# Scores of two steps taken together, their maxima subtracted by four 32-row matmuls

## The chip, the core and the metric

The kernel runs on one core of a Trainium2 chip. The core has a matrix engine (TensorE, PE in the profile; PEld is its loading of stationary operands), a vector engine (DVE), a scalar engine (ACT), GpSimd (POOL) and SyncE (SP), which mostly issues transfers. Each has an instruction stream of its own, and they wait for each other through semaphores. Matmul results go to PSUM, which has eight banks per partition. The metric is the device time of one execution in microseconds (us).

## The reference

The program is a chain of four blocks, each added to its input after a layer norm: an attention, a mixture of experts, a second attention with a position bias, and a two-layer local-attention transformer. The change touches the first one only, here in short:

```python
x = L0_attn_x                                        # 2 x 1024 x 128, float32
n = layernorm(x)
Q = (n @ Wq.T).reshape(2, 1024, 8, 64)               # 8 heads of 64
K = (n @ Wk.T).reshape(2, 1024, 8, 64)
V = (n @ Wv.T).reshape(2, 1024, 8, 128)
attn = softmax(einsum('bnhr,bmhr->bhnm', Q, K))      # 1024 x 1024 per batch and head
x = x + layernorm(einsum('bhnm,bmhd->bnd', attn, V))
```

There is no scale and no mask in this attention. The softmax is taken as the exponential of the score less its row's maximum, divided by the sum of these exponentials.

## The kernel before

`phase1` computes this block. Operands are kept as a high and a low float16 part, so a product is three matmuls: high by high, high by low, low by high.

Heads are taken in pairs, since a head has 64 rows of contraction and two fit into the 128 partitions: `rows` (line 320) is rows 0 to 63 for head e=0 and 64 to 127 for e=1. There are two batches and four pairs per batch, which makes eight `pair`s; each has two halves of 512 queries, which makes 16 units `u`; each unit has eight steps, so there are 128 steps. The pieces of work are:

- `project` (line 293) makes Q or K of a pair: six matmuls of 512 columns into one PSUM tile `big`, an ACT pass for the high part and a DVE pass (line 272) for the low part, both reading that tile. `values_of` (line 306) makes V of a pair for 512 tokens: twelve matmuls of 256 columns into a `big` tile, then ACT (line 214) and DVE (line 215) in the same way.
- `maxima` (line 322) takes rough scores of 128 queries against 512 keys, for both heads, by one matmul per head (line 329) into a `big` tile, and DVE reduces it to negated row maxima (line 332). After the eighth, `negated` (line 336) combines the halves and writes them, divided by 64, to columns 0 and 64 of a mostly zero tile `mz`. `as_rows` (line 344) transposes `mz` by four matmuls with an identity and copies the result to `mrow`: head 0's negated maxima in row 0, head 1's in row 64, zeros elsewhere.
- `scores` (line 351) takes the scores of 128 keys (step j of the unit) against the 512 queries, for both heads: eight matmuls (line 360), in pairs of one per head. The last pair multiplies `ones` (64 everywhere) with `mrow` and so adds the negated maxima. ACT takes the exponential into `p` (line 364) and casts it to the high part in `hl` (line 366); POOL subtracts for the low part (line 367).
- `values` (line 370) multiplies the eight `hl` tiles of a unit with V for 128 queries of one head: 24 matmuls of 129 columns (lines 49 to 51) into the tile `pu`. `accumulate` (line 382) takes the reciprocal of the sums in column 128 (line 387) and adds the scaled result to `acc` (lines 390 and 392), both on DVE.

PSUM is divided so: three buffers of two banks for `big`, one bank for `pu`, one for `sm`. A buffer is taken again when its last reader is done. `p` has three buffers, `hl` eighteen.

The order is set by the loop at line 420. At step m it queues `scores` of m, then `maxima` so that they run 12 steps ahead, then `values` and `accumulate` of step m - 9, then at some m `as_rows` (m modulo 8 is 4), `project` (m modulo 16 is 1 or 3) and `values_of` (m modulo 16 is 13 or 15), and pieces of other work: the second batch's tokens, and from step 80 on the preparation of the second stage (`tick`). `queue` (line 144) makes everything that a call issues come, on each engine, after what the calls before it issued; within a call a scheduler sets the order. The nine steps after the 128th have only `values` and `accumulate`.

Of the kernel before, what the change touches and what calls it, by code (L numbers as in the profile page):

```python
# [10 lines left out]
F32 = mybir.dt.float32  # L11
F32R = mybir.dt.float32r
F16 = mybir.dt.float16
BF16 = mybir.dt.bfloat16
I32 = mybir.dt.int32
AF = mybir.ActivationFunctionType
ALU = mybir.AluOpType
# [12 lines left out]
class Core:  # L30
# [7 lines left out]
    def pool(self, name, bufs, side, **kw):  # L38
        return self.tc.tile_pool(name=name, bufs=bufs, side=side, reuse_waits="tile", **kw)
# [194 lines left out]
def phase1(k, X):  # L234
# [5 lines left out]
    nc, A = k.nc, k.A  # L240
    H, R = 8, 64
    QSCALE = 16.0
    MSCALE = 64.0
    with ExitStack() as es:
# [5 lines left out]
        pp = pool("p1p", 2)  # L250
# [4 lines left out]
        big = lambda: ps_big.tile([128, 2, 512], F32, name="big")  # L255
# [10 lines left out]
        mz = [wp.tile([128, 4, 128], F16, name=f"mz{i}") for i in range(2)]  # L266
        ones = wp.tile([128, 128], F16, name="ones")
# [6 lines left out]
        S = {}  # L274

        def tokens(b):
            xn = tp.tile([128, NT, D], F32, name="xn")
            xTh, xTl = x2.tile([128, N], F16, name="xTh"), x2.tile([128, N], F16, name="xTl")
            for c in range(2):
                src = X[:, NT * b + 4 * c : NT * b + 4 * c + 4, :]  # L280
                dst = [xn[:, 4 * c + t, :] for t in range(4)]
                if b:
                    yield from k.ln_steps(x2, dst, lambda t: src[:, t, :])
                    continue
                k.ln_to(x2, dst, lambda t: src[:, t, :], *k.ln_stats(x2, lambda t: src[:, t, :], 4, False))
                s = slice(512 * c, 512 * c + 512)
                hi, _ = k.split_r(xTh[:, s], xTl[:, s], k.transposed(ps_sm, xn, c))
                S["first"] = S.get("first", hi)
            for c in range(2 * b):
                yield from k.transposed_steps(ps_sm, xn, c, xTh, xTl)  # L290
            S["x", b] = xTh, xTl
# [28 lines left out]
        rows = (slice(0, 64), slice(64, 128))  # L320

        def maxima(n):

            u, i = n // 8, n % 8
            pair, t, c = u // 2, 4 * (u % 2) + i // 2, i % 2
            qh, kh = S["q", pair][0], S["k", pair][0]
            ps = big()
            for e, r in enumerate(rows):
                nc.tensor.matmul(ps[:, e, :], qh[r, 128 * t : 128 * t + 128], kh[r, 512 * c : 512 * c + 512], start=True, stop=True)  # L329
            if i == 0:  # L330
                S["n", u] = up.tile([128, 4, 2, 2], F32, name="nm")
            S["red"] = nc.vector.tensor_reduce(S["n", u][:, i // 2, c, :], ps, AX.X, ALU.max, negate=True)  # L332
            if i == 7:
                negated(u)

        def negated(u):

            nm = S.pop(("n", u))
            nb = up.tile([128, 4, 2], F32, name="nb")
            nc.vector.tensor_tensor(nb, nm[:, :, 0, :], nm[:, :, 1, :], ALU.min)  # L340
            nc.vector.tensor_scalar(mz[u % 2][:, :, 0:128:64], nb, 1.0 / MSCALE, None, ALU.mult)

        def as_rows(u):
            z = mz[u % 2]
# [5 lines left out]

        def scores(n):

            u, j = n // 8, n % 8
            pair, c = u // 2, u % 2
            (qh, ql), (kh, kl), m = S["q", pair], S["k", pair], S["m", u]
            ks, qs = slice(128 * j, 128 * j + 128), slice(512 * c, 512 * c + 512)
            st = big()
            for i, (l, r) in enumerate(((kh, qh), (kh, ql), (kl, qh), (ones, m))):
                for e, d in enumerate(rows):
                    nc.tensor.matmul(  # L360
                        st[:, e, :], l[d, :] if i == 3 else l[d, ks], r[d, :] if i == 3 else r[d, qs], start=i == 0, stop=i == 3
                    )
            p = pp.tile([128, 2, 512], F32, name="p", bufs=3)
            S["exp"] = nc.scalar.activation(p, st, AF.Exp, scale=QSCALE**-2)  # L364
            hl = pp.tile([128, 2, 2, 512], F16, name="hl", bufs=18)
            nc.scalar.copy(hl[:, 0], p)  # L366
            S["lo"] = nc.gpsimd.tensor_tensor(hl[:, 1], p, hl[:, 0], ALU.subtract)  # L367
            S["p", n] = hl

        def values(n):  # L370
            u, i = n // 8, n % 8
# [28 lines left out]
        steps = B * H // 2 * 16  # L400
# [19 lines left out]
        for m in range(steps + lag):  # L420
            if m == 0:
                while done < 8:
                    k.queue(maxima, done)
                    done += 1
                k.queue(as_rows, 0)
                k.behind(scaled, wvh, wvl, wv, VSCALE)
            if m < steps:
                k.queue(scores, m)
            if m == 12:
                k.side.append(tokens(1))  # L430
            while m == 49 and k.side:
                k.aside()
            if m == 101:
                projecting.close()
            while done < min(steps, m + 1 + ahead):
                k.queue(maxima, done)
                done += 1
            if 0 <= m - lag < steps:
                k.queue(values, m - lag)
                k.queue(accumulate, m - lag)  # L440
            if m % 8 == 4 and m + 4 < steps:
                k.queue(as_rows, m // 8 + 1)
            if m % 16 in (1, 3) and m // 16 + 1 < B * H // 2:
                k.queue(project, m // 16 + 1, m % 16 // 2)
            if m in (2, 4):
                k.queue(values_of, 0, m // 2 - 1)
            if m % 16 in (13, 15) and m // 16 + 1 < B * H // 2:
                k.queue(values_of, m // 16 + 1, m % 16 // 2 - 6)
            if k.side:
                k.aside()  # L450
            elif 80 <= m < 86 or m >= 101 and m % 2 == 0:
                k.queue(k.tick)
# [1041 lines left out]
def tile_kernel(ctx: ExitStack, tc: tile.TileContext, A, out, first=1, last=4):  # L1494
# [33 lines left out]
    k.exp_tables()  # L1528
    k.later = []
    gens = [f(k, X) for f in (phase1, phase2, phase3, phase4)[first - 1 : last]]  # L1530
    ready = [False] * len(gens)

# [145 lines left out]
```

## Time and profile before

| what | us |
|---|---|
| median of three runs (lowest, highest) | 1354.97 (1350.28, 1356.17) |
| the profiled execution | 1356.68 |
| its span, first to last instruction | 1354.9 |
| start to the first `values` | about 62 |
| first `values` to the end of the last | about 409 |
| the rest, stages two to four | about 884 |

| 62 to 471 us of the span | PE | PEld | DVE | ACT | POOL |
|---|---|---|---|---|---|
| busy us of 409 | 381.4 | 258.6 | 263.8 | 301.2 | 274.3 |

The mean granted TensorE clock was 0.98 of full speed in this stretch and 0.945 over the span. In the profile a line of the first kind names the source line, the engine, the operation, what it writes and reads by the program's names, shapes, and how often; then busy time, the mean duration in ns, and the engine's idle time just before with what ended it. A line in order of time has start and duration in us first. Matmuls overlap in the pipeline, so their starts, not their durations, tell how fast they follow each other. A form such as `64*128` after MATMUL gives the rows and columns of the array that the matmul uses.

### The profile page before, as it was taken

What the parts mean: (1) busy time and instruction counts of PE and PEld (TensorE: products, weight loads), DVE (VectorE), ACT (ScalarE), POOL (GpSimd) and SP (SyncE); (2) the same over time, 40 slices, a digit from 0 to 9 for tenths busy, and PEclk for the clock granted to TensorE, in tenths of its full rate; (3) what the DMA queues carried; (4) which work ended last, traced back from release to release, by engine and by line L of the source; (5) the groups of instructions that cost most, each with busy time, mean ns of one, the idle gap of its engine ahead of it and who ended that gap; (6) DMA issues with size and microseconds to landing.
All of it is one profiled execution on the core that took longest, in us unless ns stands there. A gap on an engine that the chain in (4) does not pass through costs nothing.

```text
span 1354.9 us, 28455 instructions
## 1 busy us (share of the span) xinstructions
PE 1162.4 (86%) x11558; PEld 716.5 (53%) x11558; DVE 982.3 (72%) x1970; ACT 958.2 (71%) x1481; POOL 842.6 (62%) x525
## 2 busy tenths in 40 slices
PE   4799999999897889887799998798668898998886
PEld 1366666666565646443355544343336565666564
DVE  6777666776674385989888789571578887888855
ACT  2777777787686364541898987789367788887755
POOL 1666667777665463733676768785577886666611
PEclk8899999999898999998999999898679899999999
DMA  2000000000000031300000013000157666555520
GB/s 77 1 2 2 2 2 1 2 17 18 1 1 2 18 131 32 112 13 4 3 5 3 5 38 73 1 21 1 24 94 163 122 119 106 103 99 100 106 59 16
DMA packets 123394, 57.59 MB, mean 43 GB/s; under 512 B 105568, under 2 KB 114800, under 8 KB 123264
## 3 DMA queue, kind: packets, MB, share of 16 engines
q1 hardware_dynamic: 121360, 54.50, 18.7%
q8 instruction: 90, 1.47, 0.4%
q10 hardware_dynamic: 1472, 1.09, 0.3%
q0 software_dynamic: 432, 0.20, 0.2%
q14 instruction: 40, 0.33, 0.1%
HBM read 21.69 MB, written 1.11 MB: 17 GB/s over the span
## 4 chain that ended last, share of the span: by engine, by line
PE 42%; DVE 29%; ACT 14%; issue 6%; POOL 4%; DMA 3%; SPq 0%; POOLq 0%; DVEq 0%; ACTq 0%
DVE mx L869 5%; PE big L360 5%; PE pu L49 4%; PE pu L51 3%; PE pu L50 3%; DVE nm L332 3%; PE pu L920 3%; ACT pt L898 2%; PE big L49 2%; PE big L51 2%; PE big L50 2%; PE bank L895 1%; PE bank L860 1%; PE big L656 1%; DVE ln_st L81 1%
## 5 line engine op out<-in xcount | busy, mean ns | idle before, releaser
L367 POOL TENSOR_TENSOR hl<-p,hl 128x1024 f16<-128x1024 f32 x128 | 274.0, 2143 | 142.8 <-ACT hl L366 116.2
L903 POOL TENSOR_TENSOR hl<-pt,hl 128x2048 f16<-128x2048 f32 (+1 forms) x48 | 164.4, 3432 | 78.1 <-ACT hl L902 68.4
L332 DVE TENSOR_REDUCE nm<-big 128x2 f32<-128x1024 f32 x128 | 155.2, 1220 | 32.3 <-PE big L329 31.6
L364 ACT ACTIVATE p<-big 128x1024 f32<-128x1024 f32 x128 | 130.9, 1023 | 52.4 <-PE big L360 51.6
L49 PEld LDWEIGHTS <-hl 128*128 128x128 f16 x1024 | 100.5, 98 | 75.7 <-DVE acc L392 43.6
L366 ACT CAST hl<-p 128x1024 f16<-128x1024 f32 x128 | 133.8, 1045 | 4.1
L869 DVE TENSOR_REDUCE mx<-bank 128x1 f16<-128x512 f32 (+3 forms) x157 | 102.1, 653 | 32.1 <-PE bank L860 16.4
L869 DVE TENSOR_REDUCE mx<-bankz 128x1 f16<-128x512 f32 (+3 forms) x147 | 96.6, 660 | 18.7 <-PE bankz L864 12.8
L898 ACT ACTIVATE pt<-bank 128x512 f32<-128x512 f32 (+1 forms) x172 | 97.0, 582 | 18.5 <-PE bank L897 11.1
L49 PE MATMUL pu<-V1h,hl 128*128 128x129 f16 x512 | 92.6, 224 | 12.4 <-DVE acc L392 11.7
L49 PE MATMUL pu<-V0h,hl 128*128 128x129 f16 x512 | 93.1, 224 | 10.8 <-DVE acc L392 9.5
L50 PEld LDWEIGHTS <-hl 128*128 128x128 f16 x1024 | 101.3, 99 | 0.0
L1221 POOL TENSOR_TENSOR rot<-rot,rn 128x512 f32<-128x512 f32 x64 | 66.3, 1056 | 55.8 <-DVE rn L1211 50.4
L51 PEld LDWEIGHTS <-hl 128*128 128x128 f16 x1024 | 100.5, 98 | 0.0
L1196 POOL TENSOR_TENSOR rot<-rot,t 128x512 f32<-128x512 f32 x64 | 84.1, 1326 | 20.2 <-DVE t L1190 20.1
L51 PE MATMUL pu<-V0h,hl 128*128 128x129 f16 x512 | 92.5, 223 | 0.0
L50 PE MATMUL pu<-V0l,hl 128*128 128x129 f16 x512 | 92.5, 222 | 0.0
L51 PE MATMUL pu<-V1h,hl 128*128 128x129 f16 x512 | 92.0, 222 | 0.0
L50 PE MATMUL pu<-V1l,hl 128*128 128x129 f16 x512 | 92.0, 221 | 0.0
L898 ACT ACTIVATE pt<-bankz 128x512 f32<-128x512 f32 (+1 forms) x132 | 76.8, 583 | 20.8 <-PE bankz L897 9.9
L88 POOL TENSOR_TENSOR ln_rstd<-ln_rs,nhalf 128x4 f32<-128x4 f32 (+2 forms) x29 | 32.8, 1135 | 81.4 <-DVE ln_rs L84 67.3
L895 PE MATMUL bank<-qst,kz 128*128 128x512 f16 (+3 forms) x218 | 68.1, 345 | 13.5 <-DVE mx L869 7.5
(412 smaller groups left out, 3730.9 us busy)
## 6 DMA issues: line engine op xcount, KB each, us to landing
sb<-sd SPq DMA_DIRECT2D x16, 512.0 KB, 4.4
Vs<-V SPq DMA_DIRECT2D x60, 130.0 KB, 2.4
work<-in_t_w SPq DMA_DIRECT2D x2, 512.0 KB, 3.5
out<-F SPq DMA_DIRECT2D x3, 256.0 KB, 2.3
X<-in_L_attn_x SPq DMA_DIRECT2D x2, 256.0 KB, 3.3
w<-in_t_wqk SPq DMA_DIRECT2D x1, 512.0 KB, 5.1
wv<-in_t_wv ACTq DMA_DIRECT2D x1, 512.0 KB
X<-in_L_attn_x ACTq DMA_DIRECT2D x1, 512.0 KB, 5.0
```

The source lines that it names most:

```text
L49: mm(out, lh, rh, start=start, stop=False, **kw)
L50: mm(out, lh, rl, start=False, stop=False, **kw)
L51: mm(out, ll, rh, start=False, stop=stop, **kw)
L332: S["red"] = nc.vector.tensor_reduce(S["n", u][:, i // 2, c, :], ps, AX.X, ALU.max, negate=True)
L364: S["exp"] = nc.scalar.activation(p, st, AF.Exp, scale=QSCALE**-2)
L366: nc.scalar.copy(hl[:, 0], p)
L367: S["lo"] = nc.gpsimd.tensor_tensor(hl[:, 1], p, hl[:, 0], ALU.subtract)
L869: S["max"] = nc.vector.tensor_reduce(out, ps[:, :, :n], AX.X, ALU.max, negate=True)
L895: nc.tensor.matmul(st[:, a, :w], kz[:, a0 + a, 128 * j : 128 * j + 128], q1[:, s : s + w], start=True, stop=not diag)
L898: S["exp"] = nc.scalar.activation(pt[:, a0 : a0 + m, :w], st[:, :, :w], AF.Exp)
L903: nc.gpsimd.tensor_tensor(hl[:, 1, :, :w], pt[:, :, :w], hl[:, 0, :, :w], ALU.subtract)
L1196: eng("ra" if j else "rb", i).tensor_tensor(rot[:, j], rot[:, j], t2[:, j], ALU.add)
```

## The change

`scores` is now called at even steps only and does the work of two. It takes two `big` tiles. First come the matmuls that put the negated maxima into them: for each head and each of the two steps one matmul of `ones` by `mrow` over 32 rows, rows 0 to 31 and 64 to 95 for the first step, 32 to 63 and 96 to 127 for the second, each group at its own row position of the array. Then come the six score matmuls of the first step, its exponential, cast and subtraction, and the same of the second step. For this `negated` writes each maximum twice, to columns 0, 32, 64 and 96 of `mz`, so that `mrow` has them in rows 0, 32, 64 and 96.

```diff
-            nc.vector.tensor_scalar(mz[u % 2][:, :, 0:128:64], nb, 1.0 / MSCALE, None, ALU.mult)
+            twice = mz[u % 2][:, :, 0:128:32].rearrange("p t (e i) -> p t e i", e=2)
+            nc.vector.tensor_scalar(twice, nb.unsqueeze(3).to_broadcast([128, 4, 2, 2]), 1.0 / MSCALE, None, ALU.mult)
...
-            ks, qs = slice(128 * j, 128 * j + 128), slice(512 * c, 512 * c + 512)
-            st = big()
-            for i, (l, r) in enumerate(((kh, qh), (kh, ql), (kl, qh), (ones, m))):
-                for e, d in enumerate(rows):
-                    nc.tensor.matmul(
-                        st[:, e, :], l[d, :] if i == 3 else l[d, ks], r[d, :] if i == 3 else r[d, qs], start=i == 0, stop=i == 3
-                    )
-            p = pp.tile([128, 2, 512], F32, name="p", bufs=3)
-            S["exp"] = nc.scalar.activation(p, st, AF.Exp, scale=QSCALE**-2)
-            hl = pp.tile([128, 2, 2, 512], F16, name="hl", bufs=18)
-            nc.scalar.copy(hl[:, 0], p)
-            S["lo"] = nc.gpsimd.tensor_tensor(hl[:, 1], p, hl[:, 0], ALU.subtract)
-            S["p", n] = hl
+            qs = slice(512 * c, 512 * c + 512)
+            st = [big() for _ in range(2)]
+            for e in range(2):
+                for i in range(2):
+                    d = slice(64 * e + 32 * i, 64 * e + 32 * i + 32)
+                    nc.tensor.matmul(st[i][:, e, :], ones[d, :], m[d, :], start=True, stop=False, tile_position=(d.start, 0))
+            for i in range(2):
+                ks = slice(128 * (j + i), 128 * (j + i) + 128)
+                for l, r in ((kh, qh), (kh, ql), (kl, qh)):
+                    for e, d in enumerate(rows):
+                        nc.tensor.matmul(st[i][:, e, :], l[d, ks], r[d, qs], start=False, stop=l is kl)
+                p = pp.tile([128, 2, 512], F32, name="p", bufs=3)
+                S["exp"] = nc.scalar.activation(p, st[i], AF.Exp, scale=QSCALE**-2)
+                hl = pp.tile([128, 2, 2, 512], F16, name="hl", bufs=18)
+                nc.scalar.copy(hl[:, 0], p)
+                S["lo"] = nc.gpsimd.tensor_tensor(hl[:, 1], p, hl[:, 0], ALU.subtract)
+                S["p", n + i] = hl
...
-            if m < steps:
+            if m < steps and m % 2 == 0:
                 k.queue(scores, m)
```

## The prediction

> **What bounds the kernel now.** I read the page first, then busy time by stretch, then the first stage in order of time, and the order in which the changed program's instructions stand. The page:
>
> ```profile
> span 1354.9 us, 28455 instructions
> ...
> PE 1162.4 (86%) x11558; PEld 716.5 (53%) x11558; DVE 982.3 (72%) x1970; ACT 958.2 (71%) x1481; POOL 842.6 (62%) x525
> ...
> L332 DVE TENSOR_REDUCE nm<-big 128x2 f32<-128x1024 f32 x128 | 155.2, 1220 | 32.3 <-PE big L329 31.6
> L364 ACT ACTIVATE p<-big 128x1024 f32<-128x1024 f32 x128 | 130.9, 1023 | 52.4 <-PE big L360 51.6
> L366 ACT CAST hl<-p 128x1024 f16<-128x1024 f32 x128 | 133.8, 1045 | 4.1
> ```
>
> The exponential (L364) waits for the scores matmuls and hardly anything waits for it. By stretches (columns: PE, PEld, DVE, ACT, POOL busy, granted clock, DMA share, GB/s) the middle of stage one is PE's, at the full clock:
>
> ```profile
> 240.00:320.00 80.00, 77.28 (x929) 50.55 (x928) 58.51 (x108) 64.96 (x72) 62.14 (x31) 1.00 0.05 15
> ```
>
> One step, in order of time (start, duration): end of one values block, scores, maxima, next values block.
>
> ```profile
> 305.20 0.22 PE L51 MATMUL pu<-V0h,hl 128*128 128x129 f16 x1
> 305.35 0.39 PE L360 MATMUL big<-qh,kh 64*128 64x512 f16 x2
> 305.58 0.38 PE L360 MATMUL big<-ql,kh 64*128 64x512 f16 x2
> 305.79 0.38 PE L360 MATMUL big<-qh,kl 64*128 64x512 f16 x2
> 306.01 0.38 PE L360 MATMUL big<-mrow,ones 64*128 64x512 f16 x2
> 306.23 0.38 PE L329 MATMUL big<-kh,qh 64*128 64x512 f16 x2
> 306.54 0.23 PE L49 MATMUL pu<-V0h,hl 128*128 128x129 f16 x1
> ```
>
> Starts tell the price, since durations overlap. Two 64-row matmuls share one slot of 0.217. A values block is 24 matmuls 0.0575 apart, 1.32 from first to last start. From 128 rows to 64, 0.15 pass where 0.0575 would do; back, 0.31 where 0.217 would do: each change of row tiling costs 0.093. The step is 1.32+0.15+0.66+0.22+0.31 = 2.66. Counted so from first to last values block, the stage is 377.0 of the measured 407.6; nearly all undisturbed steps fit within 0.02. The rest is waits, 18 of it in six steps where stage two's preparation sits in DVE's queue.
>
> What the step hides is seen where stage one ends and only values are left:
>
> ```profile
> 453.71 0.22 PE L51 MATMUL pu<-V1h,hl 128*128 128x129 f16 x1
> 453.97 0.17 DVE L387 RECIPROCAL ri<-pu 128x1 f32<-128x1 f32 x1 [5.09 <-PE pu L51]
> 454.18 0.35 DVE L392 SCALAR_TENSOR_TENSOR acc<-pu,ri,acc 128x128 f32<-128x128 f32 x1
> ...
> 454.58 0.23 PE L49 MATMUL pu<-V1h,hl 128*128 128x129 f16 x1 [0.65 <-DVE acc L392]
> ```
>
> `pu` has one buffer, so 0.87 lie between the last start of a values block and the next block's first. In the step above scores and maxima fill 1.34, more than 0.87.
>
> The release of a projection's PSUM buffer is the second thing hidden (here `values_of`; `project` releases by L272 at the same 3.84):
>
> ```profile
> 277.64 0.22 PE L51 MATMUL pu<-V0h,hl 128*128 128x129 f16 x1
> 277.69 0.27 PE L49 MATMUL big<-wvh,xTh 128*128 128x256 f16 x1
> ...
> 279.10 0.39 PE L360 MATMUL big<-qh,kh 64*128 64x512 f16 x2
> 279.20 1.01 ACT L214 CAST V1h<-big 128x1024 f16<-128x1024 f32 x1 [0.65 <-PE big L51]
> ...
> 280.25 1.23 DVE L215 TENSOR_TENSOR V1l<-big,V1h 128x1024 f16<-128x1024 f32 x1 [1.80 <-ACT V1h L214]
> ```
>
> It comes free at 281.48, 3.84 after the values block's last start; 3.90 with 0.06 to the waiting matmul.
>
> **The change part by part**, over the 59 two-step periods between the first and last values block.
>
> *The slot saved.* Two steps had two slots for `ones`·`mrow`; four 32-row matmuls side by side need one. But the scheduler has put all four next to each other in only 32 of the 59; in 27 the second step's two follow behind scores of the first. Saving 32×0.217 = 6.9. Bounds: 0 (four overlap no better than two) to 6.9; two 64-row matmuls do share a slot fully, so I take 6.9. PE's instruction count, and the six score matmuls per step, stay.
>
> *Row-tiling changes.* 32 rows are a third mode. A period with the four together gains one change (128-32-64-128), a split one three: 32+27×3 = 113; twelve fall away late, where a step has lost both scores and maxima. 101×0.093 = +9.4. No row of before shows 64 against 32; bounds 0 (+0) and 0.2 (+20), twice the row; I take the row of 64 against 128.
>
> The Trainium skill, "TensorEngine Tiling (Array Packing)", Key Properties, speaks against the change here: it says that changing the tiling mode, not just the tile, drains the array. The rows agree that a change costs, 0.093; the page prices nothing, so by its rule alone the sum would only gain a positive term of unknown size. "TensorE: Matmul & The Clock Gate", Part 3, gives 3.07 times for four row tiles instead of 4, by which (an estimate) the saving would be some 2 smaller. Neither figure is used below.
>
> *The accumulate wait.* Scores now stand before every second values block. In the other gap PE has only maxima, 0.15+0.31 = 0.46, and must wait till 0.87. By the new order: 37 gaps with maxima alone, 37×0.41 = 15.2; 12 with the four `as_rows` matmuls too (0.69 filled), 12×0.18 = 2.2; 3 with nothing, 3×0.81 = 2.4; the few others about 1.3. Together +21.1. DVE is no later than in the quoted row: the earlier reduction (1.22) ends under the values block, the next is queued behind the accumulate. Bounds: 0 and +21.1 (a wait can't be below the DVE chain).
>
> *The buffer wait.* `big` has three buffers. After a projection (14 `values_of`, 12 `project` in the counted part) the projection and both scores tiles now hold all three, so the following maxima waits for L215 or L272 on DVE. Before, a scores and a maxima tile had the other two. Scores begin 1.46 after the last values start; with two steps in one, maxima would come at 1.46+7×0.217+0.093 = 3.07 (5 cases) or, split, at about 3.47 (21 cases), and must wait to 3.90: 5×0.83+21×0.43 = +13.2. Where dearer tiling pushes scores later, this wait shrinks by as much. Bounds 0 and +19.6 (tiling at nothing). What it displaces: DVE's delay after projections and a maxima that waits for `kh` cost before 0.2 three times and 0.3 once in 16 steps; seven times 0.9 = -6.3, now under the later PE.
>
> *At nothing.* The wider `mz` write (8 to 16 elements, L341 takes 0.18, 16 times) lies on DVE behind a reduction. Exp and cast come in pairs, 4 x 1.03 in a 5.6 period: ACT has room; POOL needs 2×2.14 = 4.3. So the rings of `p` and `hl` wait for nothing new. What the second step's scores are moved past is one maxima and one values block on PE and, on ACT, the `mrow` cast, now 2.1 later; its reader comes four steps on, and its PSUM buffer is wanted only about when it ends. No DMA is moved. The nine steps before the first values block run at ACT's pace (2.07), 0±2. SP's order is unchanged. Some ten later instructions swap places with neighbours on ACT, DVE and POOL: 0±3.
>
> *Sum:* -6.9+9.4+21.1+13.2-6.3 = +30.5. All is on PE, whose last values block opens stage two (the chain runs `pu`, `acc`, then stage two's transfer), so the span takes it whole. The profiled execution took 1356.68 (span 1354.9, 1.8 around it): 1387.2. It stands 1.7 above the median shown, 1354.97, so 1385 beside that median.
>
> **Rivals.**
> - *Tiling dearer, or the four don't overlap* (then the change doesn't do what it says). No overlap: +6.9, 1392. At 0.2 a change +20.2 instead of +9.4, the buffer wait down by 7.2 (5×0.11+21×0.32): 1389. Both 1396. For it: 32-row mode is unseen. Against: 64 and 128 behave alike both ways.
> - *Cheaper.* Tiling at nothing alone: -9.4+6.4 = -3, 1382, as the buffer wait takes it back. Buffer wait hidden alone: 1372; both: 1362. For it: L215 follows an ACT cast that could run earlier if PE's projection does. Against: the 3.84 recurs after every projection.
> - *Not slower: DVE is never last.* Both waits that I add are for DVE's releases. If PE reached the second values block later than 0.87, and the maxima later than 3.90, both go: 30.5-34.3 = -3.8, 1351. It decides only where PE takes 0.41 more per period from elsewhere, or the reciprocal and accumulate land within 0.46. Against: eight gaps of 0.87 in a row after 453.
> - *The clock.* Between 900 and 1000 it was granted at 0.74 with PE busy 74.7; full, it would return up to 74.7×0.26 = 19: 1366. Nothing in the change touches that stretch.
>
> **How the numbers follow.** Forecast case 1385 (own range 1377 to 1393): 0.64. Dearer 0.14, cheaper 0.13, DVE never last 0.05, clock 0.04. Range 1367 to 1402: dearer's 1396 with the ±5 of swaps and start on top, and below the buffer wait gone with the same ±5; it drops the two last cases and the cheap end. About 0.5% (6.8) is what a measurement here tells from no change. DVE never last is split over same and faster; the cheap end adds to same: faster 0.03, same 0.06, slower 0.91.
>
> **What would show it.** Steps alternate: gaps from values to values of 0.87 with PE waiting for DVE `acc` some 60 times in stage one, against 8 now; maxima behind a projection waiting for the DVE halves of `V` and `q`/`k` about 26 times; where the four `ones` stand together, four starts at once, then 0.31 to the first scores. Stage one some 30 longer, the rest unmoved. Wrong if PE's idle time on `acc` stays near 21, if a 32-row change costs far from 0.093, or if later stages move by over 5.

## The result and the profile after

The changed kernel takes 1388.11 us (median of four executions, 1385.74 to 1391.24), the kernel before beside it 1354.72: 1.0253 times as long, 95% interval 1.0222 to 1.0285, slower. The forecast was 1385, in a range of 1367 to 1402. The profiled execution took 1387.85.

The page of the changed kernel, the rows that answer to those of before, and the first `values` matmul:

```profile
span 1386.1 us, 28456 instructions
...
PE 1180.1 (85%) x11558; PEld 722.1 (52%) x11558; DVE 1003.3 (72%) x1970; ACT 952.3 (69%) x1481; POOL 838.1 (60%) x525
...
L332 DVE TENSOR_REDUCE nm<-big 128x2 f32<-128x1024 f32 x128 | 154.7, 1218 | 39.7 <-PE big L329 39.4
L370 ACT ACTIVATE p<-big 128x1024 f32<-128x1024 f32 x128 | 130.5, 1020 | 65.2 <-PE big L368 62.8
...
L49 PE MATMUL pu<-V1h,hl 128*128 128x129 f16 x512 | 92.6, 224 | 23.5 <-DVE acc L398 22.8
```

The counts are the same to one instruction: no matmul was saved, only placed side by side. L49 now sits idle for the accumulate. The same stretch that was shown of before, then the whole stage, and who PE waits for in it:

```profile
240.00:320.00 80.00, 74.64 (x851) 47.76 (x849) 58.80 (x101) 56.72 (x64) 52.44 (x27) 1.00 0.03 8
```

```profile
62.00:503.00 441.00, 391.54 (x4573) 259.24 (x4570) 285.04 (x510) 297.58 (x326) 270.57 (x135) 0.98 0.01 4
```

```profile
PE pu L49 <- DVE acc L398: 37.4, 58, 8.0
PE big L329 <- DVE V1l L215: 2.4, 6, 0.6
```

and the first of these of before:

```profile
PE pu L49 <- DVE acc L392: 21.2, 16, 5.2
```

(The columns are us in total, times, the longest.) In 80 us PE starts 851 matmuls instead of 929, at the full clock still. The wait for `acc` came 58 times instead of 16. The list has 21 waits of the maxima for the low halves of V, q and k; that of before has none. (In these totals, busy time runs to the modelled end of a matmul and covers part of a wait; I therefore measure waits by starts.)

The measure used from here on is the **gap**: from the last start of one values block to the first start of the next. There are 127, numbered by the block that they follow; even numbers lie behind a block of an odd head (e=1), before one of an even head, and hold what the odd step queues. Sums over gaps, in us, with `project` and `values_of` gaps apart, and those with n mod 16 = 3, in which DVE has `negated`; gaps 95 and later, where stage two's preparation runs beside, are a column of their own:

| | behind an odd head (47) | behind a projection (24) | n mod 16 = 3 (6) | other (17) | gaps 95 to 127 | stage |
|---|---|---|---|---|---|---|
| before | 75.3 | 65.7 | 8.5 | 22.7 | 64.4 | 408.9 |
| changed | 41.4 | 101.1 | 17.1 | 38.6 | 70.5 | 441.3 |

The stage is 32.3 longer. The first values block starts 1.7 later, and what follows the stage takes 880.8 instead of 883.6, so the span grows by 31.2. Over all profiled executions of this study that last part, whose code is the same in all kernels, took between 874 and 888; a single span is therefore read stage by stage, and times are compared by medians.

A two-step period with the four `ones` together, in order of time:

```profile
278.07 0.22 PE L51 MATMUL pu<-V1h,hl 128*128 128x129 f16 x1
278.22 0.39 PE L363 MATMUL big<-mrow,ones 32*128 32x512 f16 x4
278.55 0.39 PE L368 MATMUL big<-qh,kh 64*128 64x512 f16 x2
278.77 0.38 PE L368 MATMUL big<-ql,kh 64*128 64x512 f16 x2
278.99 0.38 PE L368 MATMUL big<-qh,kl 64*128 64x512 f16 x2
279.20 0.38 PE L368 MATMUL big<-qh,kh 64*128 64x512 f16 x2
279.42 0.38 PE L368 MATMUL big<-ql,kh 64*128 64x512 f16 x2
279.64 0.38 PE L368 MATMUL big<-qh,kl 64*128 64x512 f16 x2
279.89 0.39 PE L329 MATMUL big<-kh,qh 64*128 64x512 f16 x2
280.36 0.23 PE L49 MATMUL pu<-V1h,hl 128*128 128x129 f16 x1
```

Four matmuls start as one and hold one slot; from them to the first scores 0.33 pass where a slot is 0.217. The gap shown lasts 2.29, since its accumulate ended late on DVE; undisturbed, such a gap is 2.10, and 2.52 where the scheduler split the four. The gap just before it, behind an odd head:

```profile
275.88 0.22 PE L51 MATMUL pu<-V1h,hl 128*128 128x129 f16 x1
...
276.03 2.13 POOL L373 TENSOR_TENSOR hl<-p,hl 128x1024 f16<-128x1024 f32 x1 [2.58 <-ACT hl L372]
276.04 0.39 PE L329 MATMUL big<-kh,qh 64*128 64x512 f16 x2
276.14 0.17 DVE L393 RECIPROCAL ri<-pu 128x1 f32<-128x1 f32 x1 [0.26 <-PE pu L51]
276.35 0.35 DVE L398 SCALAR_TENSOR_TENSOR acc<-pu,ri,acc 128x128 f32<-128x128 f32 x1
...
276.75 0.23 PE L49 MATMUL pu<-V1h,hl 128*128 128x129 f16 x1 [0.33 <-DVE acc L398]
```

That is 0.87, with one maxima in it and PE waiting for DVE; 50 of the 59 odd-head gaps of the two-step periods are exactly so. And behind a projection:

```profile
295.86 0.22 PE L51 MATMUL pu<-V0h,hl 128*128 128x129 f16 x1
295.92 0.27 PE L49 MATMUL big<-wvh,xTh 128*128 128x256 f16 x1
...
297.43 1.01 ACT L214 CAST V1h<-big 128x1024 f16<-128x1024 f32 x1 [1.18 <-PE big L51]
...
298.48 1.23 DVE L215 TENSOR_TENSOR V1l<-big,V1h 128x1024 f16<-128x1024 f32 x1 [1.80 <-ACT V1h L214]
...
299.16 0.59 PE L368 MATMUL big<-qh,kl 64*128 64x512 f16 x2
...
299.76 0.39 PE L329 MATMUL big<-kh,qh 64*128 64x512 f16 x2
...
300.08 0.23 PE L49 MATMUL pu<-V0h,hl 128*128 128x129 f16 x1
```

The last row of scores starts at 299.16 (its second matmul at 299.37); the maxima come at 299.76, 0.05 after L215 is done with the projection's buffer (298.48+1.23) and 3.90 after the values block. With 0.32 to the next block the gap is 4.21 or 4.22, the same in every one of the 24 gaps of the table, whether the four `ones` are together or split. That is how a wait for a fixed event looks.

### The profile page after: what moved, and what is told of

Read it like the earlier page. It is cut to its first block, busy times and chain, and to the rows that moved or that the text cites. A ratio compares the mean times of both kernels' runs of the same rounds, so it can differ in the third digit from the quotient of the medians.

```text
span 1386.1 us, 28456 instructions
## 1 busy us (share of the span) xinstructions
PE 1180.1 (85%) x11558; PEld 722.1 (52%) x11558; DVE 1003.3 (72%) x1970; ACT 952.3 (69%) x1481; POOL 838.1 (60%) x525
## 4 chain that ended last, share of the span: by engine, by line
PE 44%; DVE 29%; ACT 14%; issue 6%; POOL 4%; DMA 2%; SPq 0%; POOLq 0%; DVEq 0%; ACTq 0%
PE pu L49 5%; DVE mx L875 5%; PE pu L51 4%; PE pu L50 4%; PE big L368 3%; PE pu L926 3%; ACT pt L904 2%; PE big L49 2%; DVE nm L332 2%; DVE acc L398 2%; PE big L51 2%; PE big L50 2%; PE big L662 2%; PE bank L866 1%; PE bank L901 1%
## 5 line engine op out<-in xcount | busy, mean ns | idle before, releaser
L373 POOL TENSOR_TENSOR hl<-p,hl 128x1024 f16<-128x1024 f32 x128 | 270.8, 2137 | 173.3 <-ACT hl L372 148.3
L332 DVE TENSOR_REDUCE nm<-big 128x2 f32<-128x1024 f32 x128 | 154.7, 1218 | 39.7 <-PE big L329 39.4
L370 ACT ACTIVATE p<-big 128x1024 f32<-128x1024 f32 x128 | 130.5, 1020 | 65.2 <-PE big L368 62.8
L49 PEld LDWEIGHTS <-hl 128*128 128x128 f16 x1024 | 100.7, 98 | 70.5 <-DVE acc L398 52.1
L49 PE MATMUL pu<-V1h,hl 128*128 128x129 f16 x512 | 92.6, 224 | 23.5 <-DVE acc L398 22.8
L49 PE MATMUL pu<-V0h,hl 128*128 128x129 f16 x512 | 93.5, 225 | 16.4 <-DVE acc L398 14.6
L1227 POOL TENSOR_TENSOR rot<-rot,rn 128x512 f32<-128x512 f32 x64 | 66.3, 1056 | 57.8 <-DVE rn L1217 50.2
L908 ACT CAST hl<-pt 128x2048 f16<-128x2048 f32 (+1 forms) x48 | 77.6, 1616 | 1.6 <-PE pu L926 0.2
```

What stands on the lines that cost most here:

```text
L49: mm(out, lh, rh, start=start, stop=False, **kw)
L370: S["exp"] = nc.scalar.activation(p, st[i], AF.Exp, scale=QSCALE**-2)
L908: nc.scalar.copy(hl[:, 0, :, :w], pt[:, :, :w])
```

## The experiments

The theory is that of the prediction: two waits, for the accumulate and for a projection's buffer, cost the time; the 32-row tiles themselves are nearly neutral. The rivals are that the tiles cost it, or that pairs of steps do through their bursts on ACT, POOL and DVE. Stage sums of all runs, in the columns from above:

| run | odd head | projection | mod 3 | other | 95 on | stage | ratio to before (95%) |
|---|---|---|---|---|---|---|---|
| e1_after_noacc | 28.1 | 102.6 | 19.3 | 39.4 | 64.4 | 427.6 | 1.0126 (1.0102 to 1.0149) |
| e2_before_noacc | 69.4 | 65.9 | 8.5 | 22.7 | 54.8 | 391.9 | 0.9915 (0.9893 to 0.9937) |
| e3_before_32 | 74.6 | 67.2 | 9.1 | 24.5 | 63.2 | 410.8 | 0.9998 (0.9980 to 1.0016) |
| e4_after_64 | 41.6 | 101.1 | 15.8 | 37.6 | 70.5 | 440.2 | 1.0248 (1.0221 to 1.0276) |
| e5_after_lo | 42.2 | 90.6 | 17.1 | 38.4 | 69.3 | 430.3 | 1.0177 (1.0156 to 1.0198) |
| e6_after_best | 47.1 | 77.5 | 19.4 | 34.3 | 83.3 | 434.3 | 1.0272 (1.0250 to 1.0293) |
| e7_after_apart | 57.1 | 101.1 | 11.2 | 24.8 | 63.3 | 429.9 | 1.0179 (1.0159 to 1.0198) |
| e8_after_apart2 | 63.5 | 66.3 | 11.2 | 25.1 | 68.9 | 408.0 | 0.9979 (0.9967 to 0.9991) |
| e9_best_cut | 51.6 | 75.9 | 17.4 | 33.0 | 63.0 | 412.8 | 1.0042 (1.0026 to 1.0057) |
| e10_after_cut | 65.2 | 66.4 | 9.1 | 24.8 | 63.5 | 401.3 | 0.9973 (0.9960 to 0.9986) |

### The accumulate, taken away in both kernels

```diff
-            ri = up.tile([128, 1], F32, name="ri")
-            nc.vector.reciprocal(ri, po[:, D : D + 1])
...
+            if e == 0:
+                ri = up.tile([128, 1], F32, name="ri")
+                nc.vector.reciprocal(ri, po[:, D : D + 1])
...
```

The reciprocal and the accumulate of odd heads are left out, in the changed kernel (first text) and in the kernel before (second).

> The changed kernel without the accumulation of the odd heads: the reciprocal and the scaled add of every first values block of a period are left out, so that the second block's matmuls no longer wait for DVE. The odd heads are missing from the sum, so the output is not the reference's. Theory (the wait for the one pu buffer, 0.87 from values to values, is the largest term): stage one 25 shorter than in the changed kernel, about 1363, and the gaps with maxima alone fall from 0.87 to 0.46. Rival (the loss is in the 32-row tiling and the buffers): within 4 of 1388, since neither is touched.

> The kernel before with the same accumulations of the odd heads left out (output not the reference's). Theory: only the last eight values blocks, which stand without cover, gain, four of their gaps by 0.65, and some 3 from DVE's delays: 1349 to 1353. Rival (DVE's load as a whole sets the stage, so less DVE work is worth as much here as in the changed kernel): about 1330.

Measured: 1369.62 against 1350.69 for the kernel before, and 1340.93. The plain odd-head gaps of the changed kernel fell from 0.87 to 0.47 or 0.48, as expected, and the gaps behind projections stayed at 4.21. But the time fell by less than foreseen: the odd-head gaps of the whole stage gave back 23.0 (13.3 up to gap 94, 9.7 after it), the others took 8.1 again, the values blocks 1.2, and the stage won 13.7. The kernel before won more than foreseen, 17.0 in its stage, nearly all in delays behind DVE: 1.51 became 1.34 in odd-head gaps next to projections, and gaps 95 to 127 lost 9.6. So this edit takes DVE work away beside the wait, which both kernels profit from, and the difference of the two times doesn't isolate the wait. The gaps show that the wait is there; its price needs another edit (e7).

### The tiles alone

```diff
+            for e in range(2):
+                d = slice(64 * e, 64 * e + 32)
+                nc.tensor.matmul(st[:, e, :], ones[d, :], m[d, :], start=True, stop=False, tile_position=(d.start, 0))
-            for i, (l, r) in enumerate(((kh, qh), (kh, ql), (kl, qh), (ones, m))):
+            for l, r in ((kh, qh), (kh, ql), (kl, qh)):
```

One step at a time as before, `ones` first and as two 32-row matmuls (above). And the reverse, pairs of steps as in the changed kernel with `ones` as 64-row pairs (below).

```diff
-                    d = slice(64 * e + 32 * i, 64 * e + 32 * i + 32)
-                    nc.tensor.matmul(st[i][:, e, :], ones[d, :], m[d, :], start=True, stop=False, tile_position=(d.start, 0))
...
             for i in range(2):
+                for e, d in enumerate(rows):
+                    nc.tensor.matmul(st[i][:, e, :], ones[d, :], m[d, :], start=True, stop=False)
```

> The kernel before with its two ones-by-mrow matmuls taken over 32 rows at row positions 0 and 64, and put first; one step at a time as before. It adds one change of row tiling per step, 128 in all, and saves nothing. Theory (a change to or from 32 rows costs what 64 against 128 costs, 0.093 to 0.10): 128x0.098 = 12.6 longer, 1367. Rival cheaper (free): 1355. Rival dearer (0.2): 1380.

> The changed kernel with its four ones-by-mrow matmuls as two pairs of 64 rows, as before the change, and mz with two columns; two steps are still taken together. It loses the saved slot (33x0.217 = 7) and gains back about 120 tiling changes (12), while the maxima after projections wait about 7 longer for their buffer: within 3 of the changed kernel's 1388, 1389 by the sum. Rival (32-row tiles cause the loss): 1355 to 1362.

Measured: 1350.33 against 1350.69, no change, and 1385.55, as slow as the changed kernel. In the first, an undisturbed gap went from 1.34 to 1.44: the change from 32 to 64 rows costs 0.10, as estimated. But 128 such steps would make 12.8, and the stage grew by 1.9: gaps with a wait for DVE in them absorbed it (1.51 to 1.44) or lost the wait (gap 109, 3.82 to 1.22). My theory had the mechanism and missed that cover. In the second, the plain gaps that hold the scores are 2.20, those behind an odd head 0.87 and the ones behind projections 4.21 as ever. The four-tile form is worth nothing here either way; taking two steps together costs the time. The rival of the tiles falls.

### The projection's buffer

```diff
-            scaled(hi, lo, flat(ps), QSCALE / VSCALE)
+            nc.scalar.activation(hi, flat(ps), AF.Copy, scale=QSCALE / VSCALE)
+            nc.vector.tensor_tensor(lo, hi, hi, ALU.subtract)
```

The same is done in `values_of`.

> The changed kernel, with one thing left out: the low half of the projections and of the values is written as zero (high half minus itself), so the second reader of a projection's buffer, on VectorE, is gone and the buffer comes free when ScalarE has read it. The instructions on TensorE stand in the same order. Theory (the maxima after 25 projections and value projections wait for VectorE to finish with the buffer): the gap from the values block before a projection to the next one, 4.21 us in 25 places in the changed kernel, falls to what TensorE needs there by the order of its instructions, about 3.4 where the four `ones` matmuls lie together and 3.8 where they are split, a sum of 11 to 13; the time falls from 1388 to 1375-1379, 1.015-1.018 of the kernel before. Rival (the gap is TensorE's own, or set by ScalarE's read): the gaps stay within 0.1 of 4.21 and the time within 3 of 1388. The 0.87 of the odd heads stays in both.

Measured: 1376.74, a ratio of 1.0177, as expected. The 24 gaps behind projections went from 4.21 or 4.22 to between 3.40 and 4.04, and their sum fell by 10.5; those behind an odd head did not gain (42.2 against 41.4), so it is not DVE's lighter load as such. The one shown above became:

```profile
288.07 0.22 PE L51 MATMUL pu<-V0h,hl 128*128 128x129 f16 x1
...
290.68 0.70 DVE L320 TENSOR_TENSOR V1l<-V1h 128x1024 f16<-128x1024 f16 x1 [1.80 <-ACT V1h L319]
...
291.37 0.59 PE L370 MATMUL big<-qh,kl 64*128 64x512 f16 x2
...
291.58 0.59 PE L331 MATMUL big<-kh,qh 64*128 64x512 f16 x2
...
292.10 0.23 PE L49 MATMUL pu<-V0h,hl 128*128 128x129 f16 x1
```

The row of the maxima (L331 here) follows the last row of scores by a slot, 0.21, instead of 0.60. The gap is 4.03 and not the expected 3.8, all of it PE's own: in this split order two slots hold one matmul each. The buffer wait is shown, and its price: 1388.11 less 1376.74 are 11 (10 by the ratios) of the 33, against 13.2 in the sum.

### Both waits covered by order alone

First, both maxima of a pair in the odd step, and the quads (the four `ones` matmuls of two steps) kept in line, with nothing between them:

```diff
-                k.queue(scores, m)
+                k.queue(lambda m: k.in_line(scores, m, line="scores"), m)
...
-            while done < min(steps, m + 1 + ahead):
+            while (m % 2 or m == 0) and done < min(steps, m + 1 + ahead):
```

> The changed kernel with two changes of order: the maxima of both steps are put into the odd step, behind the values of the even head, and the eight matmuls of a pair of `ones` are kept in one line, so that all 64 quads lie side by side. Everything is computed. Theory (the loss is two waits, for the accumulate of the even head with only one maxima in between, and for the buffer of a projection with the maxima right behind it): with two maxima in the gap before the odd head TensorE needs 0.68 of the 0.87 there, 0.19 is left 51 times over (10 in sum against 27 in the changed kernel); the buffer wait goes, since the maxima come one values block later; all 64 pairs save a slot of 0.217, or 14 in sum. By the same tally as in the prediction the stage is 2.5 longer than in the kernel before, 34 shorter than in the changed kernel: 1350-1358, 0.998-1.004 of the kernel before. Rival (taking two steps together costs through something else: the bursts on ScalarE, POOL and VectorE): 1370 or more.

(What this text and the next call the gap before the odd head, and the even head's accumulate, is the gap behind the odd head, and its accumulate.)

Measured: 1389.24, as slow as the changed kernel. The theory missed this outright. Block by block, though, it holds for most of the stage: up to block 90 the run is 5.7 later than before, where the changed kernel is 24.6 later (both from the first values block). It loses in two other places. The first block starts 6.8 later (what delays it stays open), and gaps from 95 on sum to 83.3 instead of 64.4. The largest, gap 109, 8.54 against 3.82 before:

```profile
444.04 0.22 PE L51 MATMUL pu<-V0h,hl 128*128 128x129 f16 x1
...
446.75 0.95 POOL L549 MEMSET work<- 128x1024 f32 x1 [1.33 <-DVE rank L547]
...
447.68 4.20 POOL L373 TENSOR_TENSOR hl<-p,hl 128x1024 f16<-128x1024 f32 x2
447.74 4.19 DVE L551 TENSOR_SCALAR work<-rank 128x64 f32<-128x64 f32 x2 [1.05 <-POOL work L549]
...
451.85 0.21 DVE L552 TENSOR_TENSOR work<-sc,work 128x64 f32<-128x64 f32 x1
451.99 0.15 DVE L393 RECIPROCAL ri<-pu 128x1 f32<-128x1 f32 x1
452.18 0.35 DVE L398 SCALAR_TENSOR_TENSOR acc<-pu,ri,acc 128x128 f32<-128x128 f32 x1
...
452.58 0.29 PE L49 MATMUL pu<-V0h,hl 128*128 128x129 f16 x1 [6.59 <-DVE acc L398]
```

Two operations of stage two on DVE, of 64 columns each, take 4.19 together; they start as POOL begins two subtractions back to back and end as these end. The accumulate is queued behind them, and PE behind the accumulate. This is a third cost, not among my steps.

Second, the quads stay, but the second step's scores go back to the odd step (`scored` holds the six score matmuls, exponential, cast and subtraction of one step):

```diff
             if m < steps and m % 2 == 0:
-                k.queue(scores, m)
+                k.queue(lambda m: k.in_line(scores, m, line="scores"), m)
+            if m < steps:
+                k.queue(scored, m)
```

and, in a further run, the maxima of the even steps behind a projection are put off:

```diff
-            while done < min(steps, m + 1 + ahead):
+            while (m == 0 or m % 16 not in (0, 2, 4, 14)) and done < min(steps, m + 1 + ahead):
```

> The four `ones` matmuls of two steps are taken together as in the changed kernel, kept in one line, but the scores of the second step, its exponentials and splits go back to the odd step; the second tile waits in its buffer with the maxima in it. Everything is computed. Theory: six matmuls of scores are again in the gap before the odd head, so the accumulate wait is gone (0.87 becomes about 1.12, TensorE's own work); a slot of 0.217 less in 64 places and a change to 32 rows of 0.10 more in 64 make 7 less than the kernel before; but the maxima now follow even closer behind a projection (one step's scores instead of two), so the buffer wait of 3.90 binds in 26 places for 38 in sum: 31 longer than the kernel before, 1378-1388, 1.017-1.026 of it. Rival (no buffer wait, or the maxima slip behind the wait): 1340-1350, 0.993-1.000.

> As the run with the second step's scores put back in the odd step, and in the even steps that follow a projection or a value projection the maxima are put off to the odd step. Everything is computed. Theory: neither the accumulate wait nor the buffer wait is left; a slot of 0.217 less in 64 pairs and a change to 32 rows of 0.10 more, 7 less than the kernel before: 1341-1347, 0.990-0.997 of it, the fastest of all runs that compute everything. Rival (the slot saved is covered by waits on VectorE, as the price of 32-row tiles was when it was paid alone): 1348-1356. Rival (holding the second tile's buffer over a values block costs a new wait on ScalarE): 1360 or more.

Measured: 1377.12 and 1350.45. They are the cleanest test, since everything is computed and only order moves. In the first, undisturbed gaps behind an odd head are 1.12 and the others 1.45: the accumulate wait is gone, and the stage is 11.4 shorter than the changed kernel's, while the gaps behind projections stand at 4.21 unmoved. The time is a shade below the expected 1378; the stage's +21 against the 31 of the tally is again the cover of waits for DVE: beyond the undisturbed length of each gap, the first 94 gaps hold 12.5 in before and about 4 here. In the second, these gaps fall to 2.54, but for most of those with n mod 16 = 11, which are 3.5 since `nb` is held under POOL there; the stage loses another 21.9, and it is 0.9 shorter than before. The time is above the expected 1341 to 1347 and where the first rival put it. Until block 80 it is 7.7 ahead, of which slots and changes make 4.7 (40×0.117); the rest is that PE waits less for DVE than in before. Then it loses 7 in gaps 83 to 109, the two largest of them (83, 3.54 against 1.37, and 109, 6.67 against 3.82) to DVE operations held under POOL like those above.

### Single steps where stage two runs beside

```diff
+    CUT = 88
...
-            if m < steps and m % 2 == 0:
+            if m < CUT and m % 2 == 0:
```

From step 88 on each step opens its own tile with two 32-row matmuls, and the maxima go back to every step. This is put on the run with both maxima in the odd step, and on the fastest one.

> The run with both maxima in the odd step and all quads in line, up to step 88; from there on one step at a time as in the kernel before (its `ones` as two 32-row matmuls in front, which cost nothing when they were paid alone). Everything is computed. Theory (two steps at a time cost what the tally says while TensorE sets the pace, and lose their time where the next stage's small VectorE operations run beside, each held as long as POOL's two subtractions that now come back to back): the first 80 values blocks stay at 4 to 5 more than in the kernel before, the last 48 lose nothing more instead of 21, the start keeps its 7: 1360-1368, 1.006-1.012 of the kernel before. Rival (the last blocks are late whatever form the scores have there): within 5 of the 1389 of the run without the cut.

> The fastest form so far (quads of `ones` in line, the second step's scores in the odd step, the maxima put off behind projections), up to step 88; from there on one step at a time as in the kernel before. Everything is computed. Theory: the 7.7 that the first 80 values blocks won stay, and the 7 that the last 40 blocks lost in two waits for VectorE behind POOL (6.67 and 4.05 us) are not lost: the stage is 7 to 9 shorter than in the kernel before, 1342-1347, 0.992-0.997 of it. Rival (the waits among the last blocks come from being early there, not from the pairs): the waits come again in the single steps, and the time is 1348-1354, 0.997-1.001.

Measured: 1357.42 against 1350.91 for the kernel before, and 1347.63. The first came out 3 below what was expected and 32 below the same form without the single steps: gaps from 95 on sum to 63.0 instead of 83.3, and what follows the stage took 874.5 instead of 883.3 in the profiled execution, which is inside its spread. The stage gives 21.5 of the 32; why the rest recurs in all four executions stays open. The second is 0.9973 of the kernel before, 0.9960 to 0.9986: slightly faster, though by less than 0.5%, and just above the expected 1342 to 1347. Its stage is 7.7 shorter. Gap 109 is 1.23 there, and the same operations of stage two, with POOL idle:

```profile
415.21 0.29 DVE L567 TENSOR_SCALAR work<-rank 128x64 f32<-128x64 f32 x2 [1.04 <-POOL work L565]
...
415.44 0.23 DVE L568 TENSOR_TENSOR work<-sc,work 128x64 f32<-128x64 f32 x1
...
416.22 2.13 POOL L387 TENSOR_TENSOR hl<-p,hl 128x1024 f16<-128x1024 f32 x1 [1.05 <-ACT hl L386]
```

They take 0.29 for two, where 4.19 stood above. With single steps gaps 95 to 127 sum to 63.0 and 63.5, as in the kernel before (64.4), so the late loss comes with the pairs and not from the place: the rival falls in both runs. That gap 109 alone is below the 3.82 of before is a matter of when its operations start: there, a DVE operation of 0.23 lasts 2.13 under one single subtraction.

## Why the prediction was right

**What bounds.** PE's order of starts carried the whole reading: by it, the stage should have grown by 30.5, and it grew by 32.3; the span by 31.2; the medians by 33.4.

**The slot and the changes of tiling (-6.9, +9.4).** Sizes right: four starts at once, one slot, 0.10 for 64 against 32 rows where 0.093 was taken from 64 against 128. Their net of +2.5 is not visible in time: e4 without them is not faster beyond its interval, and the buffer wait took back what the order of `ones` gave, since 4.21 came with quads and with split ones alike.

**The accumulate wait (+21.1).** Confirmed as 0.87 in 50 of 59 gaps, 0.48 in e1. Taking it away by order (e7, which also has all `ones` in fours) was worth 11.4 of the stage, because the buffer wait is fixed to an event: two plain gaps went from 2.10+0.87 to 1.45+1.12, but behind a projection from 4.21+0.87 to 4.21+1.12.

**The buffer wait (+13.2).** Confirmed in the gap (3.90 said and found), and 10 to 11 in time (e5).

**Displaced waits (-6.3).** The step that was mis-sized. Set against undisturbed gaps (1.34, 1.56 with `as_rows`, 2.65 or 2.63 behind projections), the first 94 gaps of before hold 12.5 more, not 6.3. Those of the changed kernel, set against 0.87, 2.10 or 2.52, and 4.21 or 4.22, hold 5.3 more, where I had expected nothing new. The net is -7.2; that it comes near -6.3 is luck. Of the 5.3, 4.5 lie in gaps n mod 16 = 3, which I had put "at nothing" with the wider `mz` write:

```profile
287.51 4.22 POOL L373 TENSOR_TENSOR hl<-p,hl 128x1024 f16<-128x1024 f32 x2 [1.59 <-ACT hl L372]
...
289.28 0.39 DVE L340 TENSOR_TENSOR nb<-nm 128x8 f32<-128x8 f32 x1
...
289.70 2.09 DVE L342 TENSOR_SCALAR mz<-nb 128x16 f16<-128x16 f32 x1
```

The write took 2.09 instead of 0.20, until POOL's second subtraction ended, and the accumulate behind it made gap 67 last 2.78 instead of 2.10. `nb` and `mz` together took 12.5 in before and 31.0 after. I had checked that POOL has room for paired subtractions, and not what waits under them.

**The last gaps and the start.** From gap 95 on the change cost 6.1, where some 4 of the sum fall there (an estimate: the terms less what undisturbed gaps make of the first 94); the start cost 1.7, within its ±2; what follows the stage moved by -2.9, within ±5.

**The rivals.** Dearer tiling falls by the 0.10; "DVE never last" by the gaps of 0.87; the clock by the 0.93 that was granted over the part behind the stage in both kernels. "Cheaper" names a real effect, the give-back between tiling and buffer wait, but e5 shows that the buffer wait itself was not hidden.

What stays open: e10 is 6.2 ahead of before at the end of the stage (7.7 less 1.5 at the start), and its median 3.3 to 3.6; the later stages' spread hides the rest.

## What to carry to other kernels

Batching two steps to save a slot changes what stands in every gap: list, for each gap, which release it covered until now (here 0.87 for a single-buffered accumulator and 3.90 for a projection's buffer) and price the gap at the larger of PE's own work and that release. The saved slots can be had without the waits when only the opening matmuls are taken together, the rest stays where it covers something, and the reader that needs a late buffer is put off: 1388 became 1350 so. And a burst on POOL is not free when POOL has room, because small DVE operations beside it can last as long as the burst.

## What the runs showed of the hardware

DVE operations on SBUF that take 0.15 to 0.20 undisturbed lasted until the POOL subtraction running at the time was done: 2.09 for one that began with the second of two subtractions, 4.19 for two that began with the first, 0.29 for the same two with POOL idle. The reduction from PSUM (L332, 1218 ns against 1220 before) and the accumulate (0.35) never stretched. The Trainium skill, "SBUF — State Buffer", Who interferes with whom, has a rule that fits: a DVE instruction with two SBUF inputs, or in a two-port mode, shares a port pair with GpSimd, and one waits for the other's whole instruction; a reduction never does. The rows agree with it; no run here shows which of the two conditions held for each operation.

The later stages, the same code in every kernel, took 874 to 888 in single profiled executions: twice the 7.7 that the best order won in its stage.
